# A four-layer attention and mixture-of-experts kernel: the early expert's results behind the routing, and its tiles outside the first attention's pools

## The chip, the core and the metric

The kernel runs on one core of one Trainium2 chip. The metric is the device time of one execution in microseconds (us), the median of several runs. The profile is of one further execution. The engines are PE (TensorE, matmuls), DVE (VectorE), ACT (ScalarE), POOL (GpSimd) and SP (SyncE, which here only issues DMAs and reads numbers into registers).

## What is computed

All is float32: x is 16 batch elements of 112 tokens with 256 features; the context is 16 times 375 rows of 256. With `ln` for the layer norm the reference is

```python
x = x + attention(ln(x), ctx_1024, ctx_1024, mask, wq, wk, wv, wo)        # 16 heads of 16
x = x + experts0(ln(x), wr, w1, b1, w2, b2)      # 8 experts, the best 2 of each token, at most 560 tokens each
x = x + plain_attention(ln(x), ctx_1024, ctx_1024, row_mask)              # one head of 256, no weights
x = x + experts1(ln(x), gate_w, w1, w2, w3)      # 8 experts, the best 2 of each token
```

and the second line, around which the change lies, is

```python
slot = jnp.where(keep, pos, cap)                 # place of a token among those of its expert
xg = x_pad[dispatch]                             # the tokens of each expert, in their order
h = _gelu(jnp.einsum('ecd,edf->ecf', xg, w1) + b1[:, None, :])
y = jnp.einsum('ecf,efd->ecd', h, w2) + b2[:, None, :]
wy = y * g[..., None]                            # g: the gate of the token for this expert
out = jax.ops.segment_sum(wy.reshape(-1, D), dispatch.reshape(-1), num_segments=T + 1)[:T]
```

An expert has 1024 hidden features, so each of its two weight matrices has 1 MB.

## The kernel before

**First attention.** It runs in 64 steps, four per batch element, each for four heads (`scores`, `least`, `exps`, `turn`, `weigh`). The order of PE, ACT and DVE is written out by hand: inside `tc.manual_schedule` a loop over `step` calls the attention's parts and, at three places of a step (0, 1, 2), whatever the table `beside` holds there; `put(step, place, f, ...)` (L781) fills it. What runs beside the attention of later elements is, for each element b: `queries_first`, `heads_first` and `output` (L546), which close its attention and store the new x to `xd`; `normed2` (layer norm; `rstd_of`, L167, does its Newton iterations for the reciprocal root either on POOL or on DVE); `routing_T`, `logits` and `first_two`. For a group of elements follow `route_a` (L588, the one-hot choices and their running count `macc`), `gates`, `route_b` (the place in the expert, by `places`, two matmuls against `macc`) and `to_slots` (L614), which scatters each token's row with POOL's indirect DMA into `xg`, the table in memory of slots per expert. Elements 12 and 13 form one group, 14 and 15 one each. After step 64 no attention is left to hide behind: PE waits for DVE, ACT and POOL of the last elements, and the steps go on to 73.

**The early expert.** After ten elements `early_choice` picks the expert with the fewest tokens. Its first 256 slots (CAPA) are complete before the others', so `early_loads` (L637) loads them (`xs`), its b2 and both its weight matrices at step 57. `early_T` turns them (step 64), `early_hidden` (L674) makes the eight pieces of the hidden layer with Gelu (steps 66 to 69, place 2), `early_result` (L687) makes two tiles y of 128 tokens, in halves of eight matmuls (steps 70 to 73), adds b2, multiplies by the gate and adds the rows to `xd` with an indirect DMA that accumulates (`add_to_tokens`, L284). Its y lies in the ring `aT` of the pool `ap`, its b2, gates and tokens in the pool `ea`. Both pools end with the first attention.

**Order of the experts.** After step 73 `ps_n` (L874) sums all counts, and `in_order` (L303) sorts the experts by count: their numbers in `idn`, overflow in `over0`. Four DVE instructions (L879, L883, "terms") then sort the biases into `b1s`.

**First experts.** The pools `fp` and `fw` and new PSUM pools stand where those of the attention stood. The loop over `at` (L981) begins with the early expert's later 192 slots (CAPB) and goes on with the others in order. `slots0` (L893) issues on SP the loads of an expert's slots and of b2; `w_in` and `w_out` (L148, L153) those of its weights; in an iteration the next expert's come in the order slots, b2, w1, w2. The weights alternate between two pools of one expert each, b2 has a ring of two, y one of four. `weights_of` makes gates and tokens on DVE, `turned0` turns the slots with PE and copies them on DVE, `hidden0` (L935) makes 16 matmuls and eight Gelus, and `result0` (L955) the tiles y. The results of an expert (`pending`) are issued behind the hidden layer of the next. `value_on` (L300) reads the expert's number from `idn` into a register of SP; seven such reads are issued here. The order in this part is the scheduler's of the framework; a DMA waits in SP's queue behind the one before it.

**Later.** The second attention reads x back from `xd` when all adds are done; nothing of that part or of the second experts is touched.

Of the kernel before, what the change touches and what calls it, by code (L numbers as in the profile page):

```python
# [21 lines left out]
KC = D // 128  # L22
# [33 lines left out]
def xattn_ffn_kernel(ctx: ExitStack, tc: tile.TileContext, a: dict, out: bass.AP):  # L56
# [279 lines left out]
        return at  # L336


    cstack = ExitStack()
    cpool = cstack.enter_context(tc.tile_pool(name="cpool", bufs=1))  # L340
    c_nat = [cpool.tile([KT, NK, D], F32, name=f"c_{b}") for b in range(B)]
    c_T = [cpool.tile([128, KC, S2], F32, name=f"cT_{b}") for b in range(B)]


    with tc.tile_pool(name="aw", bufs=1) as aw, tc.tile_pool(name="ea", bufs=1) as ea, tc.tile_pool(name="ap", bufs=2) as ap, tc.tile_pool(
        name="ps_sc", bufs=4, space=PSUM
    ) as ps_sc, tc.tile_pool(name="ps_t", bufs=3, space=PSUM) as ps_t, tc.tile_pool(
        name="ps_av", bufs=1, space=PSUM
    ) as ps_av:
        wq = aw.tile([128, KC, D], F32, name="wq")  # L350
        wk = aw.tile([128, KC, D], F32, name="wk")
        wv = aw.tile([128, KC, D], F32, name="wv")

        wo = aw.tile([128, KC, D], F32, name="wo")
        nmask = aw.tile([S, S2], F32, name="nmask")
# [190 lines left out]
        def output(b):  # L546
            oT = oTs.pop(b)
            ps = bank("ps_o")
            for k in range(KC):
                nc.tensor.matmul(ps[:S, :D], oT[:, k, :], wo[:, k, :], start=(k == 0), stop=(k == KC - 1))  # L550
            nc.vector.tensor_tensor(x[:, b, :], ps[:S, :D], x[:, b, :], ALU.add)
            based.append(nc.sync.dma_start(out=xd[b * S : (b + 1) * S, :], in_=x[:, b, :]).ins)
            mv = small.tile([S, 1, 2], F32, tag="mv2", name="mv2")
            stats(mv, 0, x[:, b, :])
            xn2[b] = mv, rstd_of(mv, 1, b + 1 < B)

        def normed2(b):
            mv, rstd = xn2[b]
# [78 lines left out]
        def early_loads():  # L637
            e = early["e"] = value_on(mybir.EngineType.SP, idfn0[0:1, 0:1], 0, E - 1)
            xs = ap.tile([128, CAPA // ST * W], F32, tag="xnT", name="xs", bufs=1).rearrange("p (j d) -> p j d", d=W)
            early["xs"] = xs  # L640
            load = nc.sync.dma_start(
                out=xs,
                in_=of_expert(xg[0:ROWS, :].rearrange("(e r) d -> e r d", e=E), e)[0:CAPA, :].rearrange(
                    "(j p) d -> p j d", p=ST
                ),
            )
            after_scatters("xg", load)

            tc.add_to_no_dep_group("xg", load.ins)
            early["b2"] = ea.tile([ST, D], F32, name="b2")  # L650
            nc.sync.dma_start(out=early["b2"], in_=a["L0_ffn_b2"][bass.ds(e, 1), :].to_broadcast([ST, D]))
            early["w"] = w_in(a["L0_ffn_w1"], e, "w1", at=0), w_out(a["L0_ffn_w2"], e, "w2", at=0)

# [11 lines left out]

        def early_gates():
            i = early["xs"]
            gate = early["gate"] = ea.tile([ST, CAPA // ST], F32, name="gate")
            token = early["token"] = ea.tile([ST, CAPA // ST], I32, name="token")
            nc.vector.scalar_tensor_tensor(gate, i[:, :, D + 2], idf0, i[:, :, D + 1], ALU.is_equal, ALU.mult)  # L670
            nc.vector.tensor_tensor(gate, gate, i[:, :, D], ALU.add)
            nc.vector.tensor_copy(token, i[:, :, D + 3])
# [14 lines left out]
        def early_result(j, f0, n):  # L687
            if f0 == 0:
                early["ps"] = ps_sc.tile([128, 512], F32, tag="sc", name="ps_ey")
                if j == 0:  # L690
                    added.append([])
            ps = early["ps"][:, :D]
            for f in range(f0, f0 + n):
                nc.tensor.matmul(
                    ps, early["hT"][f][:, j * ST : (j + 1) * ST], early["w"][1][:, f, :],
                    start=(f == 0), stop=(f == FC - 1),
                )
            if f0 + n == FC:
                y = ap.tile([128, NG * S], F32, tag="aT", name="y", bufs=4)[:, :D]
                nc.vector.tensor_tensor(y, ps, early["b2"], ALU.add)  # L700
                nc.vector.tensor_scalar(y, y, early["gate"][:, j : j + 1], None, ALU.mult)
                add_to_tokens("xd", 0, xd, early["token"][:, j : j + 1], y, added)
# [81 lines left out]
        for b in range(B):  # L784
# [12 lines left out]
            at = NG * b  # L797
            put(at + 6, 1, queries_first, b)
            put(at + 7, 2, heads_first, b)
            put(at + 8, 1, output, b)  # L800
            put(at + 9, 1, normed2, b)
            put(at + 10, 0, routing_T, b)
# [1 line left out]
            put(at + 11, 1, first_two, b)  # L804
        for g, (t0, n) in enumerate(GROUPS):
            at = NG * (t0 + n - 1) + 12
            put(at, 1, route_a, g)
            put(at + 1, 0, gates, g)
            put(at + 1, 2, route_b, g)
            for j in range(n):  # L810
                put(at + 1 + (j if n > 2 else 0), 2, to_slots, t0 + j)
# [3 lines left out]
        put(STEPS - 7, 2, early_loads)  # L815
        put(STEPS, 2, early_T)
        put(STEPS + 1, 2, early_gates)
        for f in range(FC):
            put(STEPS + 2 + f // 2, 2, early_hidden, f)
        for j in range(CAPA // ST):  # L820
            for i in range(2):
                put(STEPS + 6 + 2 * j + i, 2, early_result, j, i * FC // 2, FC // 2)

        engines = {mybir.EngineType.PE, mybir.EngineType.Activation, mybir.EngineType.DVE}
        with tc.manual_schedule(engines=engines):
# [47 lines left out]
            ps = bank("ps_n")  # L873
            nc.tensor.matmul(ps[:, :E], ones_, macc[:, B, :], start=True, stop=True)  # L874
            at = in_order(small, ps[:, :E], CAP, caps8[:, 0, :], ids0, idn0, over0, capof0, pick0)
            full = [128, E // 2, FC, E]
            for r in (slice(0, E // 2), slice(E // 2, E)):
                terms = ap.tile(full, F32, tag="s", name="terms", bufs=8)
# [7 lines left out]
    with tc.tile_pool(name="fp", bufs=2) as fp, tc.tile_pool(name="fw", bufs=2) as fw, tc.tile_pool(  # L886
# [3 lines left out]
    ) as ps_fh, tc.tile_pool(name="ps_fy", bufs=2, space=PSUM) as ps_fy:  # L890
        NT = -(-CAP // ST)

        def slots0(e, r0, rows, own=""):  # L893

            xs = fp.tile([ST, -(-rows // ST) if own else NT, W], F32, tag="xs" + own, name="xs", bufs=1 if own else 2)
            src = of_expert(xg[0:ROWS, :].rearrange("(e r) d -> e r d", e=E), e)
            full = rows // ST
            load = nc.sync.dma_start(
# [3 lines left out]
            if rows > full * ST:  # L902
                load = nc.sync.dma_start(out=xs[: rows - full * ST, full, :], in_=src[r0 + full * ST : r0 + rows, :])
                after_scatters("xg", load)
            b2 = fp.tile([ST, D], F32, tag="b2" + own, name="b2", bufs=1 if own else 2)
            of = slice(e, e + 1) if isinstance(e, int) else bass.ds(e, 1)
            nc.sync.dma_start(out=b2, in_=a["L0_ffn_b2"][of, :].to_broadcast([ST, D]))
            return xs, b2

        def turned0(xs, rows, own=""):  # L910
# [44 lines left out]
        def result0(at, hT, w2, b2, gate, token, j0, n):  # L955
            if at and j0 == 0:
                added.append([])
            for j, m in tiles(n):
                ps = ps_fy.tile([ST, D], F32, tag="y", name="ps_y")
                for f in range(FC):  # L960
                    nc.tensor.matmul(  # L961
                        ps[:m], hT[:, f, j * ST : j * ST + m], w2[:, f, :], start=(f == 0), stop=(f == FC - 1)
                    )
                y = fp.tile([ST, D], F32, tag="y", name="y", bufs=4)
                nc.vector.tensor_tensor(y[:m], ps[:m], b2[:m], ALU.add)  # L965
                nc.vector.tensor_scalar(y[:m], y[:m], gate[:m, j0 + j : j0 + j + 1], None, ALU.mult)  # L966
                rows = token[:m, j0 + j : j0 + j + 1]
# [7 lines left out]
                else:  # L975
                    add_to_tokens("xd", at, xd, rows, y[:m], added)

        nxt, (w1_next, w2_next) = slots0(early["e"], CAPA, CAPB), early["w"]
        who = [None] + [value_on(mybir.EngineType.SP, idn0[0:1, r : r + 1], 0, E - 1) for r in range(1, E)]
        pending = None  # L980
        for at in range(E):  # L981
# [571 lines left out]
```

## Time and profile before

| what | value |
|---|---|
| median of 3 runs | 1156.88 us (1152.06 to 1159.27) |
| the profiled execution | 1161.33 us |
| its span, first to last instruction | 1159.6 us, mean granted clock 0.956 |
| first attention, 15 to 397 us | PE busy 374.5 of 382.0 us |
| last steps and early expert, 397 to 425 us | PE busy 23.4 of 28.1 us, clock 0.88 |
| 425.1 to 434.6 us | PE busy 0.03 of 9.5 us |
| first experts, 434.6 to 640 us | PE busy 198.5 of 205.4 us, clock 0.98 |
| second attention and around it, 660 to 800 us | PE busy 98.0 of 140.0 us, clock 0.82 |

A timeline row has the start, the time from the first to the last of the merged instructions, engine, line, operation, output and inputs by name, their number, and in brackets the idle time of the engine before it and what ended that. Each float32 matmul stands twice in the counts of PE. In a row of windows come the stretch, its length, the busy time of the engines, the granted clock of PE (1.00 is full, 0.50 half), and the share and rate of the DMA engines. SPq rows are DMA issues; reads into registers are shown only when asked for by their line.

### The profile page before, as it was taken

To read this page: it belongs to the slowest core of one execution; us is meant where nothing else is said; L and a number is where in the kernel's file an instruction comes from. 1 tells how busy PE (TensorE), PEld (TensorE's weight loads), DVE (VectorE), ACT (ScalarE), POOL (GpSimd) and SP (SyncE) were. 2 spreads that over 40 slices of the span, in tenths; PEclk is the share of its full clock that TensorE was granted. 3 is DMA by queue.
4 is the path that set the end of the run, shared out by engine and by line. 5 is a ranking of instruction groups with operands and counts; after the bars stand their busy time and mean duration, and the time that the engine had idled before them with its cause. 6 is when DMAs were issued, how large, how long until landed. Compare 5 with 4: busy or idle time off the path is not lost. (4 is left out here: it accounts for less than half of the span.)

```text
span 1159.6 us, 17142 instructions
## 1 busy us (share of the span) xinstructions
PE 1055.3 (91%) x6268; PEld 732.0 (63%) x6268; DVE 480.0 (41%) x1810; ACT 388.5 (33%) x842; POOL 275.7 (24%) x574
## 2 busy tenths in 40 slices
PE   4999999999999969999999968668799999999997
PEld 3666666666666658865667635447568855556654
DVE  2666767767766641111112165555222222222211
ACT  1666666666656613221111144422111111110010
POOL 2010214104122231212222213323323121213331
PEclk9999999999989978999999988868899999999999
DMA  5488941001001225344443221251724224045140
GB/s 145 131 273 178 336 146 38 5 10 38 13 14 34 87 49 135 103 111 109 112 110 96 27 74 38 61 160 51 219 79 119 64 83 132 9 139 142 31 119 13
DMA packets 85714, 111.14 MB, mean 96 GB/s; under 512 B 16993, under 2 KB 76969, under 8 KB 85360
## 3 DMA queue, kind: packets, MB, share of 16 engines
q1 hardware_dynamic: 72048, 93.45, 26.0%
q0 software_dynamic: 13024, 15.94, 8.1%
q8 instruction: 53, 0.87, 0.3%
q10 hardware_dynamic: 544, 0.52, 0.2%
q14 instruction: 45, 0.37, 0.1%
HBM read 78.65 MB, written 46.04 MB: 108 GB/s over the span
## 5 line engine op out<-in xcount | busy, mean ns | idle before, releaser
L1412 PE MATMUL ps_h<-xT,v 128*128 128x256 f32 (+7 forms) x640 | 204.6, 480 | 2.5 <-DVEq L1493 1.0
L1412 PEld LDWEIGHTS ps_h<-xT,v 128*128 128x128 f32 x640 | 120.3, 191 | 83.8 <-issue 64.1
L729 ACT ACTIVATE s<-s,nmx 112x375 f32<-112x375 f32 x256 | 143.2, 604 | 15.2 <-DVE nmx L722 14.0
L722 DVE CUSTOM_DVE_ANT_0 s<-ps_s,nmask 112x375 f32<-112x375 f32 x256 | 127.9, 543 | 39.2 <-PE ps_s L714 36.5
L735 PEld LDWEIGHTS ps_at<-ident,s 112*125 112x125 f32 x768 | 99.8, 189 | 61.7 <-issue 24.8
L735 PE MATMUL ps_at<-ident,s 112*125 112x112 f32 x768 | 134.2, 297 | 4.2 <-ACT s L729 2.4
L1420 ACT ACTIVATE si<-ps_h 128x256 f32<-128x256 f32 (+7 forms) x80 | 38.4, 481 | 282.6 <-PE ps_h L1412 214.2
L961 PE MATMUL ps_y<-w,hT 128*128 128x256 f32 (+6 forms) x512 | 115.8, 380 | 0.0
L1431 PE MATMUL ps_y<-v,hT 128*128 128x256 f32 (+3 forms) x512 | 112.9, 380 | 0.0
L1421 DVE TENSOR_TENSOR hT<-ps_h,si 128x256 f32<-128x256 f32 (+7 forms) x80 | 43.7, 546 | 163.8 <-PE ps_h L1412 155.3
L944 PE MATMUL ps_h<-xsT,w 128*128 128x256 f32 (+8 forms) x320 | 104.9, 488 | 6.9 <-DMA w<-in_L_ffn_w 5.9
L1431 PEld LDWEIGHTS ps_y<-v,hT 128*128 128x128 f32 (+3 forms) x512 | 91.6, 180 | 18.9 <-issue 1.6
L961 PEld LDWEIGHTS ps_y<-w,hT 128*128 128x128 f32 (+6 forms) x512 | 89.7, 179 | 20.5 <-issue 3.4
L741 ACT COPY aT<-ps_at 125x448 f32<-125x448 f32 x128 | 67.9, 532 | 94.1 <-PE ps_at L735 88.0
L286 POOL DMA_INDIRECT xd<-y,token x34 | 52.1, 1533 | 194.1 <-DVE y L966 168.2
L951 ACT ACTIVATE hT<-ps_h,b1s 128x256 f32<-128x256 f32 (+7 forms) x72 | 41.9, 582 | 165.6 <-PE ps_h L944 140.0
L944 PEld LDWEIGHTS ps_h<-xsT,w 128*128 128x128 f32 x320 | 62.2, 199 | 46.7 <-issue 40.9
L177 POOL TENSOR_TENSOR newton<-rstd 112x1 f32<-112x1 f32 (+2 forms) x81 | 15.9, 196 | 307.1 <-DVE rstd L173 204.3
L265 POOL DMA_INDIRECT xg<-xn,dest x64 | 61.2, 956 | 82.4 <-issue 48.0
L965 DVE TENSOR_TENSOR y<-ps_y,b 128x256 f32<-128x256 f32 (+6 forms) x32 | 13.5, 423 | 130.2 <-PE ps_y L961 130.2
L751 PE MATMUL av<-aT,v 125*32 125x112 f32 x1536 | 63.7, 268 | 0.9 <-ACT aT L741 0.9
L286 POOL DMA_INDIRECT yd<-y,token x28 | 43.6, 1558 | 73.0 <-DVE y L1435 64.7
(255 smaller groups left out, 1271.6 us busy)
## 6 DMA issues: line engine op xcount, KB each, us to landing
v<-in_L_ffn_w SPq DMA_DIRECT2D x25, 1024.0 KB
w<-in_L_ffn_w SPq DMA_DIRECT2D x16, 1024.0 KB
xg<-xg SPq DMA_DIRECT2D x7, 1799.0 KB
xg<-zeros SPq DMA_DIRECT2D x1, 7168.0 KB
c<-in_ctx SPq DMA_DIRECT2D x16, 375.0 KB
xg<-zeros SPq DMA_DIRECT2D x1, 1792.0 KB
yd<-zeros SPq DMA_DIRECT2D x1, 1792.0 KB
xd<-x SPq DMA_DIRECT2D x16, 112.0 KB
```

The lines of the kernel that those rows point to most:

```text
L265: inst = nc.gpsimd.indirect_dma_start(out=slots[:, :], out_offset=bass.IndirectOffsetOnAxis(ap=rows, axis=0), in_=src, in_offset=None).ins
L286: inst = nc.gpsimd.indirect_dma_start(out=total[:, :], out_offset=bass.IndirectOffsetOnAxis(ap=token, axis=0), in_=y, in_offset=None, comp ...
L722: nc.vector.tensor_tensor_reduce(out=s, in0=ps[i], in1=nmask, scale=1.0, scalar=BIG, op0=ALU.add, op1=ALU.min, accum_out=nmx[:, i : i + 1],)
L729: nc.scalar.activation(got[2][i], got[2][i], AF.Exp, bias=got[1][:, i : i + 1], scale=-1.0)
L735: nc.tensor.transpose(pt[:KT, i * S : (i + 1) * S], s[:, c * KT : (c + 1) * KT], ident[:S, :S])
L741: nc.scalar.copy(aT, src)
L751: nc.tensor.matmul(avs[b][32 * i : 32 * i + 32, n, :], vs[b % 2][:, c, h, :], aT[:, i, :], start=(c == 0), stop=(c == NK - 1),)
L944: nc.tensor.matmul(ps[:, :n], w1[:, k, f * 128 : (f + 1) * 128], xsT[:, k, j0 * ST : j0 * ST + n], start=(k == 0), stop=(k == KC - 1),)
L961: nc.tensor.matmul(ps[:m], hT[:, f, j * ST : j * ST + m], w2[:, f, :], start=(f == 0), stop=(f == FC - 1))
L1412: nc.tensor.matmul(ps[:, :n], w[:, k, f * 128 : (f + 1) * 128], xT[:, k, j0 * ST : j0 * ST + n], start=(k == 0), stop=(k == KC - 1),)
L1421: nc.vector.tensor_tensor(hT[:, f, :n], p3[:, :n], si[:, :n], ALU.mult)
L1431: nc.tensor.matmul(ps[:m], hT[:, f, j * ST : j * ST + m], w2[:, f, :], start=(f == 0), stop=(f == FC - 1))
```

## The change

Parts: (1) The two result tiles of the early expert move from the steps 70 to 73 to behind `in_order`, before the terms. (2) Its hidden pieces move: the first from step 66 place 2 to step 65 place 1, the others over steps 66 to 70. (3) `route_a` of element 14 stands in front of `output` of 15, not behind it. (4) The reciprocal root of element 14 is made on DVE, no longer on POOL. (5) `wq`, `wk`, `wv` move to the constant pool; the early expert's b2 and second y then use `wq`'s place, its first y that of `zeros`, its later slots (`late`) that of `wk` and `wv`; gates and tokens have places of their own. Those loads need no end of the attention's pools. (6) In the expert loop w1 is issued before the slots and b2; b2 has a ring of three, y one of three.

```diff
+    wq = const.tile([128, KC, D], F32, name="wq")
+    wkv = const.tile([128, 2, KC, D], F32, name="wkv")
+    wk, wv = wkv[:, 0], wkv[:, 1]
+    late = wkv.rearrange("p a k d -> p (a k d)")[:, : -(-CAPB // ST) * W].rearrange("p (j d) -> p j d", d=W)
+    gate_e = const.tile([ST, CAPA // ST], F32, name="gate_e")
+    token_e = const.tile([ST, CAPA // ST], I32, name="token_e")
...
-        wq = aw.tile([128, KC, D], F32, name="wq")
-        wk = aw.tile([128, KC, D], F32, name="wk")
-        wv = aw.tile([128, KC, D], F32, name="wv")
...
-            xn2[b] = mv, rstd_of(mv, 1, b + 1 < B)
+            xn2[b] = mv, rstd_of(mv, 1, b + 2 < B)
...
-            early["b2"] = ea.tile([ST, D], F32, name="b2")
+            early["b2"] = wq[:, 1, :]
...
-            gate = early["gate"] = ea.tile([ST, CAPA // ST], F32, name="gate")
-            token = early["token"] = ea.tile([ST, CAPA // ST], I32, name="token")
+            gate = early["gate"] = gate_e
+            token = early["token"] = token_e
...
-                y = ap.tile([128, NG * S], F32, tag="aT", name="y", bufs=4)[:, :D]
+                y = wq[:, 0, :] if j else zeros
...
+            if b + 1 == B:
+
+                put(at + 8, 1, route_a, group_of[b - 1])
             put(at + 8, 1, output, b)
...
-            put(at, 1, route_a, g)
+            if t0 + n + 1 != B:
+                put(at, 1, route_a, g)
...
-        for f in range(FC):
-            put(STEPS + 2 + f // 2, 2, early_hidden, f)
-        for j in range(CAPA // ST):
-            for i in range(2):
-                put(STEPS + 6 + 2 * j + i, 2, early_result, j, i * FC // 2, FC // 2)
+        for f, (step, i) in enumerate(((1, 1), (2, 2), (3, 2), (4, 2), (4, 2), (5, 2), (5, 2), (6, 2))):
+            put(STEPS + step, i, early_hidden, f)
...
             at = in_order(small, ps[:, :E], CAP, caps8[:, 0, :], ids0, idn0, over0, capof0, pick0)
+            for j in range(CAPA // ST):
+                early_result(j, 0, FC)
...
-            b2 = fp.tile([ST, D], F32, tag="b2" + own, name="b2", bufs=1 if own else 2)
-            of = slice(e, e + 1) if isinstance(e, int) else bass.ds(e, 1)
-            nc.sync.dma_start(out=b2, in_=a["L0_ffn_b2"][of, :].to_broadcast([ST, D]))
+            if b2 is None:
+                b2 = fp.tile([ST, D], F32, tag="b2" + own, name="b2", bufs=1 if own else 3)
+                of = slice(e, e + 1) if isinstance(e, int) else bass.ds(e, 1)
+                nc.sync.dma_start(out=b2, in_=a["L0_ffn_b2"][of, :].to_broadcast([ST, D]))
...
-                y = fp.tile([ST, D], F32, tag="y", name="y", bufs=4)
+                y = fp.tile([ST, D], F32, tag="y", name="y", bufs=3)
...
-        nxt, (w1_next, w2_next) = slots0(early["e"], CAPA, CAPB), early["w"]
+        nxt, (w1_next, w2_next) = slots0(early["e"], CAPA, CAPB, xs=late, b2=early["b2"]), early["w"]
...
-                nxt = slots0(who[at + 1], 0, sum(CAPS0[at + 1]))
                 pool = wpool if at % 2 else fw
                 w1_next = w_in(a["L0_ffn_w1"], who[at + 1], "w1", pool, at + 1)
+                nxt = slots0(who[at + 1], 0, sum(CAPS0[at + 1]))
                 w2_next = w_out(a["L0_ffn_w2"], who[at + 1], "w2", pool, at + 1)
```

More of the change, by code (lines that the diff above doesn't have):

```diff
@@ L342, in xattn_ffn_kernel @@
     c_T = [cpool.tile([128, KC, S2], F32, name=f"cT_{b}") for b in range(B)]
-    with tc.tile_pool(name="aw", bufs=1) as aw, tc.tile_pool(name="ea", bufs=1) as ea, tc.tile_pool(name="ap", bufs=2) as ap, tc.tile_pool(
+    with tc.tile_pool(name="aw", bufs=1) as aw, tc.tile_pool(name="ap", bufs=2) as ap, tc.tile_pool(
         name="ps_sc", bufs=4, space=PSUM
@@ L891, in xattn_ffn_kernel, with slots0 @@
         NT = -(-CAP // ST)
-        def slots0(e, r0, rows, own=""):
-            xs = fp.tile([ST, -(-rows // ST) if own else NT, W], F32, tag="xs" + own, name="xs", bufs=1 if own else 2)
+        def slots0(e, r0, rows, own="", xs=None, b2=None):
+            if xs is None:
+                xs = fp.tile([ST, -(-rows // ST) if own else NT, W], F32, tag="xs" + own, name="xs", bufs=1 if own else 2)
             src = of_expert(xg[0:ROWS, :].rearrange("(e r) d -> e r d", e=E), e)
```

## The prediction

> **What bounds the kernel now.** The page comes first: PE is busy for 91% of the span, so a gain can only come from PE's idle time or from its slow clock.
>
> ```profile
> PE 1055.3 (91%) x6268; PEld 732.0 (63%) x6268; DVE 480.0 (41%) x1810; ACT 388.5 (33%) x842; POOL 275.7 (24%) x574
> ```
>
> The chain of waits covers only the last 18 us and says nothing of the place of the change, so I read PE's timeline from the end of the first attention (397 us) to the end of the first experts (665 us) for its idle entries.
>
> ```profile
> 424.85 0.29 PE L874 MATMUL ps_n<-macc,ones__71 112*128 112x8 f32 x2
> 434.61 1.07 PE L915 MATMUL ps_t<-ident,xs 128*128 128x128 f32 x4 [9.48 <-DMA xs<-xg]
> 436.08 7.80 PE L944 MATMUL ps_h<-xsT,w 128*128 128x192 f32 x32 [0.41 <-DVE xsT L916]
> ...
> 541.10 13.54 PE L944 MATMUL ps_h<-xsT,w 128*128 128x496 f32 x32 [1.42 <-DMA w<-in_L_ffn_w]
> 571.42 13.12 PE L944 MATMUL ps_h<-xsT,w 128*128 128x480 f32 x32 [2.11 <-DMA w<-in_L_ffn_w]
> 601.34 14.35 PE L944 MATMUL ps_h<-xsT,w 128*128 128x464 f32 x32 [2.15 <-DMA w<-in_L_ffn_w]
> ```
>
> Two places matter: one hole of 9.48 us before the early expert's later slots, and three waits for first-layer weights (1.42 + 2.11 + 2.15 = 5.68 us). The SP queue's timeline, and the entry for the reads of expert numbers (L301), say why.
>
> ```profile
> 432.26 0.38 SPq L898 DMA_DIRECT2D xs<-xg  x1
> ...
> 563.77 0.35 SPq L907 DMA_DIRECT2D b<-in_L_ffn_b  x1
> 564.30 0.38 SPq L150 DMA_DIRECT2D w<-in_L_ffn_w  x1
> ```
>
> ```profile
> L301 SPq TENSOR_LOAD <-idn x7: 262/263/533, 427.8 to 434.1; - x7
> ```
>
> Asked in short windows, SP runs six of the seven reads back to back from 427.8 to 431.6 us (0.9 the first, 0.62 each further one); then comes the load of the later slots, 432.26, and PE starts 2.35 us after it. The reads wait for `idn`, and that for the routing of the last batch element, which stands behind early-expert work on every engine (DVE, then POOL):
>
> ```profile
> 424.23 0.16 DVE L618 SCALAR_TENSOR_TENSOR dest<-num,pos 112x2 int32<-112x2 f32 x1
> ...
> 427.65 0.16 DVE L327 CAST idn<-ids 1x8 int32<-1x8 f32 x1
> ...
> 430.60 0.42 DVE L883 TENSOR_REDUCE b1s<-terms 128x32 f32<-128x256 f32 x1
> ```
>
> ```profile
> 422.27 1.63 POOL L286 DMA_INDIRECT xd<-y,token  x1 [4.47 <-DVE num L207]
> 425.19 0.96 POOL L265 DMA_INDIRECT xg<-xn,dest  x1 [1.29 <-issue]
> 426.46 0.95 POOL L265 DMA_INDIRECT xg<-xn,dest  x1 [0.30 <-issue]
> ```
>
> The third fact is the clock, here PE busy and granted clock in three 2-us windows: an idle of 1.93 us before 413.0 is followed by half clock.
>
> ```profile
> 411.00:413.00 2.00, 0.08 (x1) 1.00 0.05 15
> 413.00:415.00 2.00, 1.99 (x8) 0.64 0.00 0
> 415.00:417.00 2.00, 2.00 (x6) 0.51 0.03 8
> ```
>
> **The change, step by step.** I call batch elements 14 and 15 by number. In the built program the last attention steps now run as follows; all durations are the rows of before, first at full clock.
>
> *Start: a loss.* Element 14's Newton steps move from POOL (12 instructions, 398.15 to 401.39) to DVE: seven instructions, which take 1.4 us for element 15 (410.98 to 412.46). Behind them on DVE stand the routing of 12 and 13 and its tanh argument; on ACT the tanh holds back the copies of xsT. They end at 401.1 (399.66 before). PE meets the first hidden piece already here: it waits 2.8 us, runs 0.95 to 402.1. ACT must then load its Gelu table (1.28) and run one Gelu before it copies `raw`: 402.95 instead of 399.73. Yet the transposes of `raw` (L530) ran only at 402.20, since PE stood 1.93 us for POOL's Newton; now 403.55. So the loss is 1.35 us, not 3.2.
>
> *Then gains, along element 15's chain.* Between those transposes and `output` stand two hidden pieces (0.95 each) instead of four: output at 406.6 (408.33). Routing of 14 is already done, so after output's matmuls (1.0) x to xn takes 3.07 + 0.3 and xn 0.4: it ends 411.4 (413.75). Its transposes no longer sit behind two pieces at half clock: 411.45 (416.86). Logits: one hidden piece instead of half a result tile in front, 412.7 (418.85). On DVE no y is in front of the choice: from the logits' copy 0.64 to `num`, then 2.47 as before, so dest ends 416.2 (424.39). in_order follows directly, without the second y: `idn` at 418.3 (427.81). POOL scatters 0.8 after dest, two of 1.25, and packets end 1.2 us after the second: 420.4.
>
> *SP.* Two reads stand before the load now, not six: 418.3 + 1.5, plus 0.65 from the last read to the load as before: 420.45, no earlier than the scatters allow. Data 2.35 later: 422.8. The other five reads and that of `over0` come after, some 3.7 us, covered by the next step.
>
> *PE meanwhile.* The 16 result matmuls run from 415.3, 7.6 us (417.11 to 425.01 less the routing between them): 422.9. They fill the hole, and data and PE arrive together. What is late next is DVE: second y 0.8, the bias terms 2.03 (428.99 to 431.02), gates 0.9, xsT 0.6. In before all but the last lay in the hole; now they are in series, and hidden of the first expert starts at 427.35 (436.08).
>
> *Clock.* The Trainium skill, "TensorE: Matmul & The Clock Gate", section "HAM oscillation — how this bites in real kernels", says that idle gaps matter above about 3.4 us. Its windows of 3.4 us agree with the half-clock stretches here (3.41 us or multiples), its threshold does not: the rows above show half clock after 1.93 us. By the rule my gaps of 2.8, 1.5 and 2.9 us cost nothing. By the row, the first costs 1.5 us (the pieces and transposes on the chain twice as long), the second 0.85 (half of one stretch's 1.7; between 0 and 1.7), the third 1.7 within hidden. Hidden needs 5.2 us at full clock (Gelus 0.65 apart at its end) and took 7.80. By the row it starts at 429.7 and ends at 436.6; by the rule it ends at 432.55.
>
> *Next expert.* Its w1 goes out before its slots; both wait for the last bias terms, as w1's buffer lies where those pools were. Slots needed 4.8 us from issue to the first gate (434.83 to 439.65); behind 1 MB at the 370 GB/s of 442 to 446 us that is 2.8 more, 7.6. Issue is 1.2 us after the terms, so they land 8.8 after them; PE wants them at 1.5 + 6.9 = 8.4. Cost 0.4, between 0 and 2.8 (by the rule, which lets hidden end earlier, 2.1). With the transposes and two result matmuls (2.1 as before), expert 1's hidden starts at 439.1 instead of 446.19: **7.1 us** gained (9.4 by the rule).
>
> *Loop.* In before b2 (L907) waits for the last y of two experts earlier, for want of a third place, and w1 stands behind it on SP: issued at 564.30, wanted at 569.3. With a third place and w1 first, the w1 for that expert waits for the hidden of two experts earlier and, in the queue, for the w2 ahead of it, which needs the results of three earlier (end near 534): about 35 us of lead against the 7.1 it took. All three waits go: **5.68 us**. The slots, b2 and w2 behind it have at least a hidden (13 us) of lead. After the third wait the clock was half for 3.4 us: 14.35 for 464 columns, where 13.12 x 464/480 is 12.7. I count half of these 1.65, **0.8**, since two of three waits had no such stretch.
>
> *At nothing:* b2, the late slots, gates and y in other places move no work; the weights w_q, w_k, w_v load as before. Three places for y instead of four: a y may wait for the landing of the one three tiles back, 10.5 us earlier at 3.5 a tile; the longest delay of an add was 7.4 us, so it holds, but with little to spare (below).
>
> Sum: 7.1 + 5.7 + 0.8 = 13.6. The profiled execution (1161.3, span 1159.6) would become 1147.7 and 1146.0; it lies 4.4 above the median. From the median 1156.9: **1143.3 us** (1141.0 by the rule).
>
> **Rivals.** (1) *The front gain is given back* to DVE's series, to the clock and to slots behind w1; only the loop gains. For it: every gap named is short of one clock window only by luck, and DVE's order is fixed. Against: the hole is 9.5 us, and the chain to `idn` is shorter by 9.5. Time 1156.9 - 6.5 = 1150.4. (2) *The loop's waits stay*: the reordered w1 meets a wait of its own, on PE or on the queue, and the change doesn't do what it says there. Against: the built order has w1 wait only on matmuls long over. Time 1156.9 - 7.1 = 1149.8. (3) *Slower: three places for y.* Adds are held when weights fill the DMA engines (7.4 us at worst, before). If, with weights issued at other times, an add is late by more than 10.5 - 1.6 - 1.5 = 7.4 us, the fourth y waits; PE itself stops only when both banks of ps_y stand unread, some 7 us later. So it decides from about 15 us of lateness, twice what any row shows. At 20 us in five four-tile experts it costs 25: 1156.9 - 13.6 + 25 = 1168.
>
> **How the numbers follow.** Forecast 0.76, (1) 0.10, (2) 0.10, (3) 0.04. The forecast's own range: clock by the rule and no slot wait, 4.4 better (1139), with the profile's full 1.65 and a start 2 us shorter 1136; all bounds against me (0.85 and 2.4 more, and 3 for a chain I have shortened too much), 1149. The whole range reaches over (1) and (2): 1136 to 1152. What a measurement of this kernel tells from no change is about 1%, 11.6 us, so faster by more than that is 1145.3 or less: nine tenths of the forecast and a fifth of (1) and (2), 0.72; same 0.24; slower 0.04.
>
> **What would show it.** In the changed profile the result matmuls of the early expert stand as one block after ps_n, and the hole before the later slots' transposes is under 1.5 us; a gap of about 3 us released by DVE follows. `idn` is 8 to 10 us earlier, two reads precede the load. No weights wait over 0.5 us in L944's successor. Half-clock stretches between 400 and 435 are shorter than before's 20 us. I am wrong if the reads or the scatters still release the later slots long after PE is done, if the slots of expert 1 land more than 2 us late, or if PE waits for DVE's y.

## The result, and the profile after

| | before | changed |
|---|---|---|
| median of 4 runs each | 1157.15 us (1152.06 to 1159.27) | 1143.52 us (1141.87 to 1144.41) |
| ratio | | 0.9887, 95% interval 0.9853 to 0.9921 |
| the profiled execution, its span, mean clock | 1161.33, 1159.6, 0.956 | 1143.56, 1141.8, 0.959 |

The medians differ by 13.6 us, and 13.6 us were forecast. The interval allows 9 to 17 us, so stage times have to say whether the steps were right too. First the page of the changed kernel, and the entries of its PE timeline at the places that were shown of before (the lines of the program are shifted: L874, L915 and L944 of before are now L881, L926 and L955):

```profile
PE 1054.8 (92%) x6268; PEld 731.9 (64%) x6268; DVE 480.7 (42%) x1817; ACT 388.1 (34%) x842; POOL 272.9 (24%) x562
```

```profile
396.17 2.08 PE L687 MATMUL ps_eh<-xsT,w 128*128 128x256 f32 x4 [2.84 <-ACT xsT L668]
...
411.95 0.36 PE L246 MATMUL ps_p<-m,before 112*112 112x8 f32 x2 [1.52 <-DVE m L221]
...
412.37 0.37 PE L881 MATMUL ps_n<-macc,ones__71 112*128 112x8 f32 x2
412.59 8.84 PE L700 MATMUL ps_ey<-w,hT 128*128 128x256 f32 x32
421.95 0.70 PE L926 MATMUL ps_t<-ident,wkv 128*128 128x128 f32 x4 [0.52 <-DVE wq L706]
425.88 7.12 PE L955 MATMUL ps_h<-xsT,w 128*128 128x192 f32 x32 [3.24 <-issue]
...
525.50 13.47 PE L955 MATMUL ps_h<-xsT,w 128*128 128x496 f32 x32
553.48 13.04 PE L955 MATMUL ps_h<-xsT,w 128*128 128x480 f32 x32
581.01 12.62 PE L955 MATMUL ps_h<-xsT,w 128*128 128x464 f32 x32
```

PE's busy time is the same to 0.5 us; what went is idle time. The hole of 9.48 us before the late slots (`wkv` is their new place) is 0.52, the result matmuls stand in it as one block, and the three large hidden layers wait for no weights. What is new is the idle of 3.24 us before the first hidden layer. The row says "issue", but the DVE timeline shows what PE stood for: the copy of `xsT` ends at 425.79, and everything ahead of it since the last result is in series.

```profile
415.51 0.16 DVE L327 CAST idn<-ids 1x8 int32<-1x8 f32 x1
...
421.47 0.42 DVE L706 TENSOR_TENSOR wq<-ps_ey,wq 128x256 f32<-128x256 f32 x1 [2.64 <-PE ps_ey L700]
...
423.82 0.42 DVE L892 TENSOR_REDUCE b1s<-terms 128x32 f32<-128x256 f32 x1
...
425.18 0.61 DVE L927 COPY xsT<-ps_t 128x256 f32<-128x256 f32 x2
...
432.59 0.23 DVE L941 SCALAR_TENSOR_TENSOR gate<-xs,ids 128x4 f32<-128x4 f32 x1 [6.81 <-DMA xs<-xg]
```

On SP the late load goes out at 418.55 behind two of the seven reads of expert numbers, and in the loop w1 goes ahead of b2:

```profile
418.55 0.38 SPq L908 DMA_DIRECT2D wkv<-xg  x1
...
424.45 0.41 SPq L150 DMA_DIRECT2D w<-in_L_ffn_w  x1
...
523.10 0.42 SPq L150 DMA_DIRECT2D w<-in_L_ffn_w  x1
525.57 0.35 SPq L918 DMA_DIRECT2D b<-in_L_ffn_b  x1
```

**Stages.** Starting times of two executions can't be subtracted as they stand. The two kernels compute the same up to the end of the first attention, yet in the profiled execution of the changed one the last `weigh` matmul of that attention starts 4.95 us earlier (392.73 against 397.68). Of this, 0.9 stood by 319 us; 2.9 came with a half-clock stretch of 6.8 us in before near 320 us; and 1.1 came near 372 us, nearly all of it a step that a1 (the new front) takes as before does and b1 (the old front) does not. So these 4.95 of the 17.8 us between the spans are not counted as the change's. The table counts from the start of the early expert's transposes (`early_T`), which no version here moves, and then in separate pieces; "expert 1" is the first whole expert of the loop.

| kernel | to `ps_n` | to late transposes | to first hidden (192 slots) | to expert 1's hidden | from there to expert 7's | second attention to the end |
|---|---|---|---|---|---|---|
| before | 27.70 | 37.46 | 38.93 | 49.04 | 193.60 | 484.63 |
| changed | 20.17 | 29.75 | 33.68 | 42.47 | 186.27 | 485.72 |
| a1_front_only | 18.79 | 28.37 | 32.31 | 41.44 | 193.00 | 489.05 |
| a2_loop_only | 27.71 | 37.53 | 39.12 | 48.75 | 185.92 | 485.82 |
| a3_terms_first | 18.92 | 28.50 | 30.03 | 39.61 | 186.13 | 484.36 |
| a4_b2_ring_only | 26.06 | 35.75 | 37.36 | 47.64 | 185.95 | 486.38 |
| b1_order_only | 24.34 | 34.46 | 36.12 | 45.77 | 186.23 | 489.03 |
| b2_results_back | 25.53 | 33.16 | 34.66 | 44.10 | 185.63 | 485.11 |
| b3_late_in_pool | 20.17 | 34.94 | 36.50 | 46.29 | 186.49 | 485.00 |
| b4_newton_pool | 16.53 | 26.11 | 29.80 | 38.98 | 186.66 | 489.15 |
| c0_changed_again | 21.38 | 29.69 | 33.22 | 42.00 | 186.02 | 486.30 |
| c1_slots_first | 21.41 | 29.78 | 31.38 | 42.70 | 187.49 | 489.99 |
| c2_filler | 17.90 | 26.18 | 29.74 | 38.52 | 187.26 | 484.52 |
| c3_all | 17.90 | 26.18 | 27.86 | 39.01 | 189.11 | 486.40 |

Between these two executions the change brought 49.04 - 42.47 = 6.57 us in front and 193.60 - 186.27 = 7.33 us in the loop, together 13.9. The loop's figure repeats: 185.6 to 187.5 with the loop of the change or one edit of it (189.1 in c3, where the first layer of the stage runs in part at half clock), 193.0 and 193.6 without. The front's doesn't. Four kernels have the front of before (before, a2, a4 and b1; what differs in them lies in the loop), and they take 45.77 (b1) to 49.04 us (before) to expert 1's hidden. All four have the same two idles of 1.9 us ahead of `ps_n`; behind them stand two half-clock stretches of 3.4 us in before and a2, one in a4 and none in b1, and `ps_n` comes at 27.7, 26.06 and 24.34. Here is b1's second idle, with full clock behind it:

```profile
405.76 0.36 PE L246 MATMUL ps_p<-m,before 112*112 112x8 f32 x2 [1.93 <-DVE m L221]
```

```profile
406.00:408.00 2.00, 2.00 (x13) 1.00 0.04 8
```

The front of the change takes 41.44 to 42.47 us (a1, c0, changed). By pairs of executions the gain in front is therefore 3.3 to 7.6 us, and 6.57 is one pair. The last column belongs to work that no version touches and lies between 484.4 and 490.0; that spread is as large as most edits, so single edits are read from their stage and the totals are kept for the whole.

### The profile page after: what moved, and what is told of

It reads as the page before. It is cut to its first block, busy times and chain, and to the rows that moved or that the text cites. A ratio compares the mean times of both kernels' runs of the same rounds, so it can differ in the third digit from the quotient of the medians.

```text
span 1141.8 us, 17142 instructions
## 1 busy us (share of the span) xinstructions
PE 1054.8 (92%) x6268; PEld 731.9 (64%) x6268; DVE 480.7 (42%) x1817; ACT 388.1 (34%) x842; POOL 272.9 (24%) x562
## 5 line engine op out<-in xcount | busy, mean ns | idle before, releaser
L955 PE MATMUL ps_h<-xsT,w 128*128 128x256 f32 (+8 forms) x320 | 102.5, 480 | 4.0 <-issue 3.2
L972 PEld LDWEIGHTS ps_y<-w,hT 128*128 128x128 f32 (+6 forms) x512 | 89.7, 179 | 20.5 <-issue 3.4
L286 POOL DMA_INDIRECT xd<-y,token x32 | 48.7, 1522 | 175.7 <-DVE y L977 170.7
L955 PEld LDWEIGHTS ps_h<-xsT,w 128*128 128x128 f32 x320 | 61.1, 195 | 41.7 <-issue 36.2
L976 DVE TENSOR_TENSOR y<-ps_y,b 128x256 f32<-128x256 f32 (+5 forms) x30 | 12.7, 423 | 131.7 <-PE ps_y L972 131.6
```

The lines of the kernel that those rows point to most:

```text
L286: inst = nc.gpsimd.indirect_dma_start(out=total[:, :], out_offset=bass.IndirectOffsetOnAxis(ap=token, axis=0), in_=y, in_offset=None, comp ...
L955: nc.tensor.matmul(ps[:, :n], w1[:, k, f * 128 : (f + 1) * 128], xsT[:, k, j0 * ST : j0 * ST + n], start=(k == 0), stop=(k == KC - 1),)
L972: nc.tensor.matmul(ps[:m], hT[:, f, j * ST : j * ST + m], w2[:, f, :], start=(f == 0), stop=(f == FC - 1))
```

## The experiments

The theory: the gain has two independent parts, the filled hole in front and the weights in the loop, and a half-clock stretch follows the short gaps in front. The rivals are those of the prediction, that the front is given back or that the loop's waits stay. Unless the text says otherwise a kernel computes all of the reference. Each was timed beside the kernel before on the same chip; "ratio" is to that.

**Front and loop apart.** a1_front_only is the changed kernel with the loop as before, a2_loop_only is before with the loop of the change.

```diff
-                b2 = fp.tile([ST, D], F32, tag="b2" + own, name="b2", bufs=1 if own else 3)
+                b2 = fp.tile([ST, D], F32, tag="b2" + own, name="b2", bufs=1 if own else 2)
...
-                y = fp.tile([ST, D], F32, tag="y", name="y", bufs=3)
+                y = fp.tile([ST, D], F32, tag="y", name="y", bufs=4)
...
+                nxt = slots0(who[at + 1], 0, sum(CAPS0[at + 1]))
                 pool = wpool if at % 2 else fw
                 w1_next = w_in(a["L0_ffn_w1"], who[at + 1], "w1", pool, at + 1)
-                nxt = slots0(who[at + 1], 0, sum(CAPS0[at + 1]))
```

> The changed kernel with the expert loop as it was before: slots and b2 ahead of w1, b2 in two places, y in four. My theory (front and loop are two separate gains): the early part stays as fast as in the changed kernel (6.6 us from the last attention matmul to expert 1's hidden layer), the three weight waits of 1.4 to 2.2 us come back, so 1157.2 - 6.6 = about 1150.5 us. Rival 'the front is given back later': about 1157. Rival 'the loop gives nothing': about 1143.5.

> The kernel before with the loop's edits alone: w1 first, b2 in three places, y in three. My theory: the hole of 9.5 us stays, the weight waits of 5.7 us go and with them half-clock time behind them, so 1157.2 - 6 to 7 = about 1150.5 us; together with the front-only kernel the gains add up to that of the whole change. Rival 'the loop gives nothing': 1157. Rival 'three places for y stall': above 1157.

Measured: a1 1153.09 us, ratio 0.9940 (0.9919 to 0.9961); a2 1151.58, ratio 0.9948 (0.9932 to 0.9965). The two parts add up to 1.1%, the whole change has 1.1 to 1.3%. The table says the same without overlap: a1 has the front of the change and the loop of before (193.00), a2 the reverse (185.92). In a1's PE timeline the loop's waits are back, with a half-clock stretch behind one of them (14.81 us where the changed kernel takes 13.04):

```profile
528.83 13.54 PE L955 MATMUL ps_h<-xsT,w 128*128 128x496 f32 x32 [0.76 <-DMA w<-in_L_ffn_w]
559.05 14.81 PE L955 MATMUL ps_h<-xsT,w 128*128 128x480 f32 x32 [2.01 <-DMA w<-in_L_ffn_w]
590.51 12.69 PE L955 MATMUL ps_h<-xsT,w 128*128 128x464 f32 x32 [1.99 <-DMA w<-in_L_ffn_w]
```

Rivals (1) and (2) fall. So does (3): with three places for y no idle of PE in the loop of the changed kernel is over 0.75 us.

**Which edit of the loop.** a4_b2_ring_only is before with the rings alone; b1_order_only is before with the order alone.

```diff
-            b2 = fp.tile([ST, D], F32, tag="b2" + own, name="b2", bufs=1 if own else 2)
+            b2 = fp.tile([ST, D], F32, tag="b2" + own, name="b2", bufs=1 if own else 3)
...
-                y = fp.tile([ST, D], F32, tag="y", name="y", bufs=4)
+                y = fp.tile([ST, D], F32, tag="y", name="y", bufs=3)
```

> The kernel before with only b2 in three places (and y in three, for space); the order of issue stays slots, b2, w1, w2. My theory: the wait of b2 for the y of two experts earlier is the whole cause of the late weights, so either edit of the loop alone takes the waits away: no weight wait over 0.5 us and about 1150.5 us, as for both. Rival 'the order is what counts': waits of 1.4 to 2.2 us stay and the time is 1157.

```diff
-                nxt = slots0(who[at + 1], 0, sum(CAPS0[at + 1]))
                 pool = wpool if at % 2 else fw
                 w1_next = w_in(a["L0_ffn_w1"], who[at + 1], "w1", pool, at + 1)
+                nxt = slots0(who[at + 1], 0, sum(CAPS0[at + 1]))
```

> The kernel before with only the order of issue changed in the expert loop: w1 ahead of slots and b2; b2 stays in two places, y in four. My theory: w1 no longer stands behind b2's wait, so the weight waits go as with the b2 ring: the loop from expert 1's hidden layer to expert 7's takes about 186 us instead of 193.6, the time is about 7 us below before's. Rival 'the ring of b2 is what counts': the loop stays at 193 us.

Measured: a4 1150.93, ratio 0.9927 (0.9908 to 0.9946); b1 1150.39, ratio 0.9935 (0.9904 to 0.9967). Each alone takes the whole: 185.95 and 186.23 us against 193.60. The two edits are redundant, which is what a queue in order gives: w1 was late only because it stood behind a b2 that waited for its place. Either w1 is ahead of it, or b2 doesn't wait. In b1's timeline of SP the b2 of the expert whose hidden starts at 528.01 (first row) still goes out late, but nothing that is wanted soon stands behind it: what follows are its w2 (L155) and the w1 of the next expert (L150), which has 29.4 us until its hidden at 555.99. In before w1 had 7.1 us.

```profile
525.48 0.35 SPq L907 DMA_DIRECT2D b<-in_L_ffn_b  x1
526.06 0.38 SPq L155 DMA_DIRECT2D w<-in_L_ffn_w  x1
526.63 0.43 SPq L150 DMA_DIRECT2D w<-in_L_ffn_w  x1
```

**The whole again**, unchanged, beside the kernels of its chip:

> The changed kernel once more, on one chip with the three that follow: 13.6 us below before, ratio 0.988.

Measured: 1146.14, before there 1160.79; ratio 0.9871 (0.9847 to 0.9895). Its front differs from the first profile of the same program (`ps_n` 21.38 against 20.17): a half-clock stretch of 10.2 us instead of 6.8 follows the same gap.

**The results put back.** b2_results_back has everything of the change but the move that its title names.

```diff
+        for j in range(CAPA // ST):
+            for i in range(2):
+                put(STEPS + 6 + 2 * j + i, 2, early_result, j, i * FC // 2, FC // 2)
...
-            for j in range(CAPA // ST):
-                early_result(j, 0, FC)
```

> The changed kernel with the two early result tiles back in the steps 70 to 73; places outside the pools and the loop as changed. My theory has most of the early gain in two things: the chain to the experts' numbers without result matmuls and y in between, and fewer reads and no pool in front of the late slots. With the results back, the counts' sum comes at about 26 us after the early transposes (20.2 in the changed kernel, 27.7 before), the late slots' transposes about 9 us after it instead of 9.6 because the reads and the load follow at once, and hidden of the first expert starts 35 to 36 us after (33.7; before 38.9). So about 2 us slower than the changed kernel. Rival 'the order is everything': it starts at 38.9 as before, 5 us slower.

Measured: 1144.37, ratio 0.9875 (0.9847 to 0.9902). `ps_n` comes 5.4 us later than in the changed kernel (4.2 than in c0), the hole is open again, and yet expert 1's hidden starts only 1.6 to 2.1 us later than in the changed kernel (44.10 against 42.47 and 42.00):

```profile
425.37 1.06 PE L927 MATMUL ps_t<-ident,wkv 128*128 128x128 f32 x4 [7.34 <-DMA wkv<-xg]
```

Behind the hole DVE has nothing left to do, so hidden follows 1.5 us after the late transposes and not 3.9. Most of the gain in front comes therefore from the other edits there: a2, which has the loop's edits alone, has the ratio 0.9948, b2 with the other front edits added 0.9875, and the intervals lie apart. Moving the matmuls into the hole and exposing DVE's series cancel in large part. In total time the move can't be told from nothing.

**The late slots back in the loop's pool.**

```diff
-        nxt, (w1_next, w2_next) = slots0(early["e"], CAPA, CAPB, xs=late, b2=early["b2"]), early["w"]
+        nxt, (w1_next, w2_next) = slots0(early["e"], CAPA, CAPB, b2=early["b2"]), early["w"]
```

> The changed kernel with the late slots back in a tile of the pool fp. Then their load waits for the last bias terms on DVE, whose buffers lie there, and for all reads. Terms end about 32 us after the early transposes; load 0.4 later, data 2.35 after it, PE's transposes, gates and xsT 1.5: hidden of the first expert at about 36.4 instead of 33.7, so 2.7 us slower than the changed kernel. Rival 'DVE sets it anyway, the place is worth nothing': 33.7, same time.

Measured: 1147.20, ratio 0.9916 (0.9890 to 0.9943). Hidden starts at 36.50 (36.4 expected), and expert 1's hidden about 4 us later than in the changed kernel (46.29). The load waits for the last term, since its place is in the pools that now begin, and goes out at 424.35 instead of 418.55; PE waits 5.71 us. The SP row and PE's:

```profile
424.35 0.38 SPq L908 DMA_DIRECT2D xs<-xg  x1
```

```profile
427.00 1.07 PE L926 MATMUL ps_t<-ident,xs 128*128 128x128 f32 x4 [5.71 <-DMA xs<-xg]
```

Here the places outside the pools are worth twice what the move of the results is, and the move needs them: with the load waiting for the terms behind the results, the hole stays open though the results have moved. The reverse does not hold, as b2 keeps most of the gain without the move.

**Newton back on POOL.**

```diff
-            xn2[b] = mv, rstd_of(mv, 1, b + 2 < B)
+            xn2[b] = mv, rstd_of(mv, 1, b + 1 < B)
```

> The changed kernel with element 14's Newton steps back on POOL. DVE's routing of 12 and 13 and with it the tanh come 1.4 us earlier, so the first hidden piece starts about 1.4 us earlier (PE's idle before it 1.4 instead of 2.8), but the layer norm of 14 comes 0.8 us later. My theory: PE then waits for that norm instead, the sum of both idles is about the same and the time is within 1 us of the changed kernel's. Rival 'moving it was a loss': 1.5 us or more faster. Rival 'moving it was a gain': 1.5 us or more slower.

Measured: 1141.88, ratio 0.9841 (0.9809 to 0.9873), the lowest of all, with an interval that overlaps those of several others. The expectation of my theory fell: `ps_n` comes 3.6 to 4.9 us earlier than in the changed kernel (16.53 against 20.17 and 21.38), expert 1's hidden 3.0 to 3.5. The first hidden piece waits half as long, and runs at full clock:

```profile
397.22 1.13 PE L687 MATMUL ps_eh<-xsT,w 128*128 128x256 f32 x4 [1.44 <-ACT xsT L668]
```

**Filling the gaps.** c2_filler adds transposes that nobody reads, in the two gaps of the changed kernel's front; nothing of the computation is left out.

```diff
+        def warm(n):
+            ps = ps_sc.tile([128, 512], F32, tag="sc", name="ps_w")
+            for i in range(n):
+                nc.tensor.transpose(ps[:, (i % 4) * 128 : (i % 4 + 1) * 128], ident, ident)
...
+        put(STEPS + 1, 1, warm, 24)
+        put(STEPS + 8, 0, warm, 12)
```

> The changed kernel with idle transposes of the identity matrix put into PE's first two gaps (24 before the first hidden piece, 12 before the places of element 15), whose result nobody reads. My theory of the clock: gaps of 2.8 and 1.5 us each bring half-clock stretches of 3.4 to 6.8 us, which cost the chain 2.4 us and the results 1.2. If the gaps are filled the stretches near 395 and 412 us go away, the counts' sum comes about 2 us earlier (18 instead of 20.2 after the early transposes) and the 16 result matmuls take 7.6 instead of 8.8: 2 to 3.5 us faster than the changed kernel. Rival 'the clock does not lie on the path there': same time within 0.5 us.

Measured: 1144.09, ratio 0.9859 (0.9836 to 0.9882), on the chip where the changed kernel had 0.9871. PE now has work in both gaps, and the result matmuls take 7.15 us instead of 8.84:

```profile
396.90 2.84 PE L683 MATMUL ps_w<-ident 128*128 128x128 f32 x24
...
411.65 1.51 PE L683 MATMUL ps_w<-ident 128*128 128x128 f32 x12
...
413.96 7.15 PE L705 MATMUL ps_ey<-w,hT 128*128 128x256 f32 x32
```

To expert 1's hidden 3.5 to 4.0 us are won (38.52); the medians on that chip lie 2 us apart (1146.14 and 1144.09), which the intervals don't tell from nothing. The second gap does not always cost: in c0 and c1 the same idle of 1.5 us stands ahead of the counts, and the result matmuls take 7.15 us too. The windows of the changed kernel show what is avoided, a granted clock of 0.50 with PE busy throughout:

```profile
395.00:397.00 2.00, 0.83 (x2) 0.75 (x3) 0.98 (x8) 1.98 (x7) 0.00 (x0) 0.72 0.00 0
397.00:399.00 2.00, 2.00 (x13) 0.93 (x12) 0.00 (x0) 1.23 (x3) 0.00 (x0) 0.50 0.00 0
```

Set beside each other, the kernels with the new front price both the gap and the clock, by the length of the half-clock stretch behind the gap (read from the granted clock in short windows) and the time to `ps_n`:

| kernel | gap before the first piece | half clock after it | to `ps_n` |
|---|---|---|---|
| b4 | 1.44 us | none | 16.53 |
| c2, c3 | filled | none | 17.90, 17.90 |
| a1, a3 | 2.85, 2.84 | 3.4 us | 18.79, 18.92 |
| changed, b3 | 2.84, 2.85 | 6.8 us | 20.17, 20.17 |
| c0, c1 | 2.84, 2.84 | 10.2 us | 21.38, 21.41 |

(b2 has the gap of 2.84 and 6.8 us of half clock; its `ps_n` stands behind the results and can't be set beside these.) Each further stretch of 3.4 us costs 0.9 to 1.4 us on this chain; Newton on DVE costs 17.90 - 16.53 = 1.4 without any clock.

**Making the first hidden layer earlier.** Its start waits for DVE's series, of which the bias terms are half. a3_terms_first puts them ahead of the results.

```diff
-            for j in range(CAPA // ST):
-                early_result(j, 0, FC)
...
-                terms = ap.tile(full, F32, tag="s", name="terms", bufs=8)
+                terms = ap.tile(full, F32, tag="aT", name="terms", bufs=4)
...
+            for j in range(CAPA // ST):
+                early_result(j, 0, FC)
```

> The changed kernel with the four bias instructions (terms) put ahead of the two early result tiles, with buffers in the ring aT. My theory says that in the changed kernel DVE's series behind the second y (0.8, terms 2.0, gates 0.9, xsT 0.6) sets the start of the first expert's hidden layer, and that DVE is idle in front of both y (1.2 and 2.6 us), where the terms would be free. So hidden starts 2.0 us earlier, w1 of expert 1 can be issued up to 2.9 us earlier, and the time is about 1141.5 us. Rival 'the late slots' load sets it': no change, 1143.5.

Measured: 1143.49, ratio 0.9866 (0.9843 to 0.9889). Hidden starts 11.1 us after `ps_n` instead of 13.5 (changed, with the same 8.84 us for the results), 2.4 us less; with results at 7.15 it is 10.0 (c1) instead of 11.8 (c0), 1.9 less. It runs at full clock (5.44). So the theory's 2.0 us hold for this step. But the total is the number of the rival (1143.5), because then PE waits for expert 1's slots, which stand behind 1 MB of w1:

```profile
423.34 5.44 PE L955 MATMUL ps_h<-xsT,w 128*128 128x192 f32 x32 [0.82 <-issue]
...
430.64 0.63 PE L926 MATMUL ps_t<-ident,xs 128*128 128x128 f32 x4 [1.86 <-DMA xs<-xg]
```

That w1 went out at 423.13 only, since the other five reads of expert numbers stood before it on SP. c1_slots_first therefore adds to a3 the old order for the first iteration alone, and c3_all adds c2's filler to that.

```diff
+                if at == 0:
+                    nxt = slots0(who[at + 1], 0, sum(CAPS0[at + 1]))
                 pool = wpool if at % 2 else fw
                 w1_next = w_in(a["L0_ffn_w1"], who[at + 1], "w1", pool, at + 1)
-                nxt = slots0(who[at + 1], 0, sum(CAPS0[at + 1]))
+                if at:
+                    nxt = slots0(who[at + 1], 0, sum(CAPS0[at + 1]))
```

> Terms ahead of the early results, and for expert 1 alone its slots and b2 again ahead of its w1. With terms first, hidden of the first expert started 2 us earlier, but PE then stood 1.9 us for expert 1's slots, which lie behind 1 MB of w1. With slots first they land 4.8 us after an issue at about 423.1, before PE wants them; w1 lands by about 430.5, when it is wanted. So 1 to 1.9 us less than terms first and 2.5 to 4 us less than the changed kernel. Rival 'the bytes are the bound, whatever their order': PE waits as long, now for w1, no gain over terms first.

> Terms first, slots of expert 1 first, and the filled gaps together. If the gains are of different stretches they add up: 4.5 to 7 us less than the changed kernel, about 1138 where before has 1157. Rival 'they hide one another': no more than the better of the two.

Measured: c1 1150.50, ratio 0.9894 (0.9864 to 0.9924); c3 1147.70, ratio 0.9882 (0.9860 to 0.9904). The slots are in time, and now w1 is late: issued at 430.41 it is used 8.8 us later, PE waits 3.74 us for it and part of the layer behind runs at half clock (8.83 us; 7.14 in before).

```profile
439.24 8.83 PE L955 MATMUL ps_h<-xsT,w 128*128 128x256 f32 x32 [3.74 <-DMA w<-in_L_ffn_w]
```

Expert 1's hidden is no earlier than in the changed kernel (42.70; in c3 39.01 where c2 alone has 38.52). My reckoning of w1's landing was wrong, and the rival holds in its outcome: slots and w1 together are late in this place in either order, so more time won ahead of them turns into a wait. Its reason is only in part shown. Between 430.41 and 439.24 the DMA engines moved 302 GB/s, an estimated 2.7 MB, so w1 shared them with the w2 issued at 430.97 and expert 2's w1 issued at 433.39; an order with those later was not tried.

## Why the prediction was right, and where it was not

The forecast's mechanism holds at the places that carry its sum, and the sizes missed in both directions. For the comparison I add 4.95 to the starts of the changed kernel.

- **The first piece** waits 2.84 us (2.8 forecast) and starts at 401.12 (401.1). The loss by DVE's Newton, forecast at 1.35 at the transposes of `raw`, is 1.32 there by c2 against b4 (6.37 and 5.05 us after the early transposes).
- **The clock after the first gap** was sized at 1.5; it cost 20.17 - 17.90 = 2.3 in the profiled execution, 0.9 to 3.5 in others. **After the second gap** 0.85 was taken between 0 and 1.7; the matmuls took 8.84, 1.69 more than with the gap filled, so it was the upper end in this execution, and nothing in c0 and c1. At full clock they take 7.15, not 7.6: before ran them at full clock too, but in three pieces with other matmuls between, and I added rows whose ends overlap those. By the rule of the Trainium skill ("TensorE: Matmul & The Clock Gate", "HAM oscillation — how this bites in real kernels"), which counts gaps above about 3.4 us, both would have been free. Every one of the seven runs with the gap of 2.84 us unfilled shows half clock behind it, and none of the three without it. The measurement decides against the rule here, but it gives no other threshold: the forecast took its row of 1.93 us for the rule, and the same idle of 1.93 us had no half clock behind it in b1. A window that runs free of the kernel, which the same page states under "What's actually happening", could explain this, and why the stretch is 6.8 us in one execution of the same program and 10.2 in another, but no run here controls its phase.
- **`idn` and the load.** `idn` ends at 415.67, that is 7.2 us earlier; 8 to 10 were forecast, without the clock. With the first gap filled (c2) it ends 9.45 us earlier, counted from the early transposes, where the working had 9.5; so the steps of the chain were right, and what it missed by is the half clock. Two reads stand before the load, as forecast, but it goes out 2.88 us after `idn`, not 2.15: 1.86 us after the last scatter's row on POOL ends, where I had 1.2 for its packets. It cost nothing, since PE came later than the data.
- **The hole** is 0.52 us (under 1.5), the gap behind it 3.24 (about 3). DVE's series from the last result matmul to hidden took 4.45, the forecast value to the hundredth.
- **Hidden** starts at 430.83 (429.7) and takes 7.12 (6.9). **Slots behind w1** cost nothing instead of 0.4: the gate (DVE's row at 432.59) shows them there 0.4 us before hidden ends. This is a narrow margin, as a3 shows, where hidden ends earlier and 1.86 us are waited. The transposes and two results took 1.67 instead of 2.1.
- **Front** in sum: 6.57 instead of 7.1; expert 1's hidden at 439.6 instead of 439.1.
- **Loop:** 7.33 instead of 6.5. The three waits of 5.68 went, and with them all of the 1.65 us of half clock, of which I had counted half. w1 goes out 30.4 us ahead of its use (523.10 against 553.48), where I had about 35.

Half clock around this part sums to 13.6 us in three stretches, against 20.5 in before: shorter, as was forecast.

So the sum came out right with terms that were off by 0.5 and 0.8 in opposite directions, and the agreement of the medians to 0.1 us is luck. More luck lies in the row of before that the front was reckoned from: it had two half-clock stretches ahead of `ps_n`, and reckoned from b1's execution of the same front the gain would have been 3.3 us smaller. In the profiled executions 1.1 us more passed behind the second attention, within what unchanged work varies.

What stays open: b4 has the best ratio, but its interval overlaps those of the changed kernel, c2 and a3. b4 with the filler or with the terms first was not tried. The moves of the hidden pieces and of `route_a`, parts 2 and 3 of the change, were never taken out alone, so what each edit brings of the shorter chain to `idn` is not shown. And why an idle of 1.5 or 1.9 us is followed by half clock in one execution and not in the next stays open.

## What to carry to other kernels

A queue in order passes one load's wait for a buffer to everything behind it: look for the small load that waits, and free it or pass it, since either does all. Work moved into a hole is worth the hole less what then stands in series behind it; here the move in the title, taken out alone, was worth some 2 us of 6.6 in single profiles, and nothing that the medians tell. Before a gain is read from one profile, look at how the same untouched part varies: 3.3 us here. An edit that makes a gap of 1.4 us into one of 2.8 in front of dense matmuls should be priced with the clock behind it, which cost 0.9 to 3.5 us here.

## What the hardware showed unexpectedly

Gaps well under 3.4 us brought half clock: 2.84 us each time (stretches of 3.4 to 10.2 us), 1.52 us in the changed kernel (3.4 us) but not in c0, the same program; 1.9 us four times in before and a2, once of two in a4, not in b1. In the loop of before 1.42 and 2.11 us brought none and 2.15 did, and in b4 1.44 us did not. The length of a gap alone does not decide, and the same program gave stretches of 6.8 and 10.2 us at the same place. Transposes that nobody reads were enough to keep the clock full: with 24 of them in the gap of 2.84 us no half clock followed (c2, c3). A load of 1 MB that was used 7.1 us after its issue in the loop of before took 8.8 us in c1, with expert 1's slots in front of it and two more loads of 1 MB behind it.
